# Output projection of a decoder layer: seven block products in place of eight, and three smaller edits around it

## The chip, the cores and the metric

The kernel runs on one core of one Trainium2 chip. The metric is device time in microseconds (us). A core has a matrix engine (PE, TensorE; the profile shows its weight loads apart, as PEld), a vector engine (DVE, VectorE), an activation engine (ACT, ScalarE), a general engine (POOL, GpSimd) and a queue engine for transfers (SP). Each works through its own queue of instructions in order and waits on semaphores for what the others produce.

## The reference

One decoder layer over 16 sequences of 256 tokens with 256 features, in f32. First a recurrent mixing block (an input product, a short convolution, a gated scan over time), then cross-attention with 8 heads of 128 columns, then a router with experts. The part that matters here is the cross-attention of one sequence, whose keys and values come from 256 latent rows (the normalised tokens themselves) and 77 context rows, 333 in all:

```python
q = x_n @ Wq + bq                      # 256 x 1024, 8 heads of 128
k, v = split(kv_in @ Wkv + bkv)        # 333 x 1024 each
p = softmax(q_h @ k_h.T / sqrt(128))   # per head, 256 x 333
o_h = p @ v_h                          # per head, 256 x 128
y = concat(o_h) @ Wo + bo + x          # 256 x 256: the output projection
x2 = layernorm(y)                      # goes to the router and the experts
```

The output projection is a product of 256 x 1024 by 1024 x 256.

## The kernel before

**Tiling and stages.** Stage A is the recurrence (`rec_in`, `rec_state`, `rec_add`, `rec_out`), for batches in pairs or fours. Stage B is the cross-attention, head by head. Stage C is the expert part, from about 1040 us on. A prologue loads weights, normalises the context and prepares batch 0.

**The loop over heads.** Stage B is one loop over 128 heads (16 batches by 8). Iteration i issues keys and queries of head i (`head_kq`, L573), then a list of extra steps for this (batch, head), then the product of scores and values of head i-2 (`head_out`, L624), the scores and softmax of head i (`head_softmax`, L589), the turning of the scores of head i-1 (`head_turn`, L608: TensorE transposes L617, copied by VectorE at L619 and by ScalarE at L620), and a second list of steps. A step of the first list is entered by `at(b, h, step, ...)`, one of the second by `behind(b, h, step, ...)`. These lists hold everything that is not a head: recurrence products, preparation of the next batch, projection, normalisation, router. A scheduler keeps dependences and decides from this order how each engine's queue is laid out; `tc.issue_after(x)` makes what is issued in its block come after x.

**The projection.** The head outputs of a batch are kept transposed in `ot` (128 x 8 heads x 256 tokens). For a batch b-1, `project` (L643) runs at (b, 2) for tokens 0 to 127 and at (b, 3) for tokens 128 to 255. Each half is 8 f32 products, one for each head, summed in half of one PSUM bank `pw`: the weights are the 128x128 block of `ot`, the moving operand is `wo_s[:, h, :]` of 256 columns (L649). In hardware one f32 product is two pairs of weight load and matmul, so a batch has 32 pairs. After the second half, GpSimd has added the bias to the tokens (`xb`, L663), VectorE adds `pw` and `xb` into `y` (L665), and `layernorm` (L139) takes its statistics and writes the normalised rows back into `xs` (L150). In batch 15, whose projection comes after the last head, each half is normalised by itself (`norm_half`).

**The neighbours that the change touches.** `prep_norm` (L487) makes the normalised rows `zl` of the next batch: four small GpSimd operations give the scale, then two VectorE operations (L492) multiply. It stands at (b, 2) for even next batches and (b, 0) for odd ones. `prep_keys` (L495) transposes `zl` and writes `kvt` (L506). `prep_values` (L533) already computes the values with seven products over blocks, in banks `pv`. `settle` (L686) scales a finished batch into `o` and sends it out. In the recurrence, `rec_in` convolves `hp` into `cv` (L336 to L338), takes its tanh into `th` (L341), and multiplies (L343). `load_rest` (L287) loads the projection's weights `wo_s`, 1 MB, by one transfer on SP in the prologue. Pools named b1, b2, a2 give tiles of one or two buffers.

Of the kernel before, what the change touches and what calls it, by code (L numbers as in the profile page):

```python
# [10 lines left out]
F32 = mybir.dt.float32  # L11
I32 = mybir.dt.int32
AF = mybir.ActivationFunctionType
ALU = mybir.AluOpType
# [4 lines left out]
P = 128  # L19
B, S, D = 16, 256, 256  # L20
# [6 lines left out]
KC = 4  # L27
H, DH = 8, 128
# [10 lines left out]
def decoder_layer(  # L39
# [28 lines left out]
    nc = tc.nc  # L68
    V, A, G, T = nc.vector, nc.scalar, nc.gpsimd, nc.tensor

    PB = 2
    PT = PB * S
# [11 lines left out]
    def bank(name, tag="mm", bufs=2):  # L84
        return ps.tile([P, 512], F32, tag=tag, bufs=bufs, name=name)
# [27 lines left out]
    part = cpool.tile([P, 2], F32, tag="part", name="part")  # L113
# [25 lines left out]
    def layernorm(dst, src, n, rows, name):  # L139

        mv = small.tile([P, n, 2], F32, tag="mv", name=f"mv{name}")
        for i in range(n):
            st = small.tile([P, 6], F32, tag="st", name=f"st{name}_{i}")
            V.bn_stats(st[:rows], src[:rows, i, :])
            V.bn_aggr(mv[:rows, i, :], st[:rows])
        v = small.tile([P, n], F32, tag="v", name=f"v{name}")
        V.tensor_scalar(v[:rows], mv[:rows, :, 1], EPS, None, ALU.add)
        r = rsqrt(v, n, rows, name)
        for i in range(n):
            V.tensor_scalar(  # L150
                dst[:rows, i, 0:D], src[:rows, i, :], mv[:rows, i, 0:1], r[:rows, i : i + 1], ALU.subtract, ALU.mult
            )
        return mv, r
# [28 lines left out]
    gl = wpool.tile([P, DC], F32, tag="gl", name="gl")  # L182
    bl = wpool.tile([P, DC], F32, tag="bl", name="bl")
    emb_s = wpool.tile([P, DC, E], F32, tag="emb", name="emb_s")
    wsum = wpool.tile([P, 4, 512], F32, tag="wsum", name="wsum")
# [126 lines left out]
    sums, yss, xs, stats = {}, {}, {}, {}  # L312

    def rec_in(pr, c, i=None):

        if c == 0 and pr > 0:
            hss[pr] = hs_tile(f"hs{pr}")
            sums[pr] = aw.tile([P, PT], F32, tag="sums", bufs=2, name=f"sums{pr}")
        a, n = (0, PB) if i is None else (i, 1)
        cols = slice(a * S, (a + n) * S)  # L320
        ph = bank(f"ph{pr}_{c}")[:, 0 : n * S]
        for k in range(DC):
            T.matmul(
                ph,
                lhsT=inw[:, k, c * P : (c + 1) * P],
                rhs=xTs[pr][:, k, cols],
                start=(k == 0),
                stop=(k == DC - 1),
            )
# [12 lines left out]
        hs = hss[pr]  # L342
        V.scalar_tensor_tensor(hs[:, c, cols], th, 1.0, z, ALU.add, ALU.mult)  # L343
# [51 lines left out]
    ysums, normed = {}, {}  # L395
# [25 lines left out]
    zs, kvts, vs, outs_t = {}, {}, {}, {}  # L421
# [62 lines left out]

    stages, kvt_ends = {}, {}

    def prep_norm(b):  # L487
# [153 lines left out]
    pws, norms, xbs = {}, {}, {}  # L641

    def project(b, i):  # L643

        ot = outs_t[b]
        if i == 0 or b == B - 1:
            pws[b] = bank(f"pw{b}_{i}")
        for h in range(H):
            T.matmul(  # L649
                pws[b][:, i * D : (i + 1) * D],  # L650
                lhsT=ot[:, h, i * P : (i + 1) * P],
                rhs=wo_s[:, h, :],
                start=(h == 0),
                stop=(h == H - 1),
            )
# [8 lines left out]
        y = b2.tile([P, 2, D], F32, tag="yb", name=f"yb{b}")  # L664
        V.tensor_tensor(y.rearrange("p i d -> p (i d)"), pws.pop(b), xb.rearrange("p i d -> p (i d)"), ALU.add)  # L665
        norms[b] = layernorm(xs[b], y, 2, P, f"b{b}")

    def norm_half(b, i):

# [24 lines left out]

    def settle_now(b):
        r2 = again(*norms.pop(b), f"o{b}")
        o = b2.tile([P, 2, D], F32, tag="yb", name=f"o{b}")
# [162 lines left out]
    for b in range(B):  # L860
        nb = b + 1
        new_pair = nb % PB == 0 and nb < B
        if b > 0:
            early = 2 * int(b == B - 1)
            at(b, 2, project, b - 1, 0)
            at(b, 3 - early // 2, project, b - 1, 1)
            at(b, 5 - early, turn_tokens, b - 1)
            at(b, 6 - early, score_experts, b - 1)
            at(b, 6 - early, choose, b - 1)
            at(b, 7 - early, dispatch, b - 1)  # L870
            at(b, 7, settle, b - 1)
        if new_pair:
            if nb == PB:
                at(b, 0, rec_state, nb, nb + 1)
            elif nb % 4 == 0:
                at(b, 0, rec_state, nb, nb + 3)
            at(b, 1, rec_add, nb, PB)
            at(b, 1, rec_out, nb)
            at(b, 2, prep_norm, nb)
            at(b, 3, rec_out, nb + 1)  # L880
            at(b, 3, prep_keys, nb)
            at(b, 3, prep_sums, nb)
            for n, h in enumerate((4, 6, 7)):
# [388 lines left out]
```

## Time and profile before

| what | value |
|---|---|
| median of 3 runs | 1182.75 us (1182.72 to 1184.29) |
| profiled execution, its own time | 1185.1 us |
| its span in the trace | 1183.4 us |
| PE busy | 1153.7 us, 5100 matmuls |
| weight loads busy | 830.1 us, 5100 loads |
| VectorE busy | 758.0 us, 2251 instructions |
| ScalarE busy | 486.7 us, 1284 instructions |
| GpSimd busy | 312.4 us, 564 instructions |
| matmuls of the projection (L649) | 512, a mean of 379 ns each from start to end |
| weight loads of the projection | 512, a mean of 190 ns each |

The profile is that of one execution, which lay 2.35 us above the median of the runs. "Busy" is the time in which an engine has at least one instruction under way; matmuls overlap, so the mean duration of one is longer than the distance from one to the next. A row of a group names the line, the engine, the operation, the tiles written and read, the shapes, the count, then busy time and the mean of one in ns, then the engine's idle time before them and who ended it. A row of a timeline gives the start of a run of equal instructions, the time from the first start to the last end, and their number; idle time before it stands in brackets.

### The profile page before, as it was taken

To read this page: it belongs to the slowest core of one execution; us is meant where nothing else is said; L and a number is where in the kernel's file an instruction comes from. 1 tells how busy PE (TensorE), PEld (TensorE's weight loads), DVE (VectorE), ACT (ScalarE), POOL (GpSimd) and SP (SyncE) were. 2 spreads that over 40 slices of the span, in tenths; PEclk is the share of its full clock that TensorE was granted. 3 is DMA by queue.
4 is the path that set the end of the run, shared out by engine and by line. 5 is a ranking of instruction groups with operands and counts; after the bars stand their busy time and mean duration, and the time that the engine had idled before them with its cause. 6 is when DMAs were issued, how large, how long until landed. Compare 5 with 4: busy or idle time off the path is not lost. (4 is left out here: it accounts for less than half of the span.)

```text
span 1183.4 us, 15727 instructions
## 1 busy us (share of the span) xinstructions
PE 1153.7 (97%) x5100; PEld 830.1 (70%) x5100; DVE 758.0 (64%) x2251; ACT 486.7 (41%) x1284; POOL 312.4 (26%) x564
## 2 busy tenths in 40 slices
PE   7999999999999999999999999999999999999996
PEld 3565677767777777677777777677777778876654
DVE  6655768676747674856467757756466564656665
ACT  3344444443444443444444434444344443523331
POOL 2211133222211321222113322222122212144544
PEclk9999999999999999999999999999999999999998
DMA  7740101000100010000000100000001000145752
GB/s 236 233 142 30 38 19 36 20 29 28 37 11 25 20 43 16 27 29 18 15 10 23 36 14 10 19 14 15 10 14 45 14 9 4 30 154 142 184 156 85
DMA packets 46617, 60.35 MB, mean 51 GB/s; under 512 B 7925, under 2 KB 36574, under 8 KB 46536
## 3 DMA queue, kind: packets, MB, share of 16 engines
q1 hardware_dynamic: 39158, 50.05, 13.4%
q0 software_dynamic: 6048, 9.22, 3.0%
q8 instruction: 40, 0.66, 0.2%
q14 instruction: 41, 0.34, 0.1%
q10 hardware_dynamic: 1330, 0.10, 0.1%
HBM read 36.07 MB, written 30.78 MB: 56 GB/s over the span
## 5 line engine op out<-in xcount | busy, mean ns | idle before, releaser
L631 PE MATMUL po<-ptt,v 128*128 128x256 f32 (+1 forms) x768 | 191.6, 383 | 1.5 <-DVE ptt L619 1.5
L631 PEld LDWEIGHTS po<-ptt,v 128*128 128x128 f32 (+1 forms) x768 | 141.8, 190 | 56.3 <-issue 29.8
L596 DVE TENSOR_REDUCE nm<-s 128x2 f32<-128x666 f32 x128 | 108.3, 846 | 93.1 <-PE s L594 93.1
L579 PE MATMUL pk<-kvt,wkv_s 128*128 128x333 f32 x512 | 164.9, 444 | 0.0
L594 PE MATMUL s<-kt,qt 128*128 128x333 f32 x512 | 164.3, 442 | 0.0
L600 ACT ACTIVATE p<-s,nm 128x333 f32<-128x333 f32 x256 | 135.3, 534 | 40.4 <-DVE nm L596 36.3
L639 ACT ACTIVATE ot<-po,bkv_s 128x256 f32<-128x256 f32 x128 | 60.6, 473 | 192.4 <-PE po L631 191.3
L584 PE MATMUL pq<-kvt,wq_s 128*128 128x256 f32 x512 | 131.2, 378 | 0.0
L579 PEld LDWEIGHTS pk<-kvt,wkv_s 128*128 128x128 f32 x512 | 91.1, 191 | 45.3 <-issue 22.5
L594 PEld LDWEIGHTS s<-kt,qt 128*128 128x128 f32 x512 | 96.4, 189 | 31.1 <-issue 0.5
L584 PEld LDWEIGHTS pq<-kvt,wq_s 128*128 128x128 f32 x512 | 96.7, 189 | 30.5 <-issue 0.5
L649 PE MATMUL pw<-wo_s,ot 128*128 128x256 f32 x512 | 115.9, 379 | 0.0
L620 ACT COPY ptt<-pb 77x256 f32<-77x256 f32 x128 | 47.0, 368 | 165.0 <-PE pb L617 162.3
L649 PEld LDWEIGHTS pw<-wo_s,ot 128*128 128x128 f32 x512 | 97.0, 190 | 13.2
L605 DVE TENSOR_SCALAR pn<-p,rs 128x333 f32<-128x333 f32 x256 | 100.0, 426 | 3.8
L835 POOL DMA_INDIRECT xg<-xs,sidx x64 | 65.4, 1022 | 92.4 <-DVE sidx L832 61.6
L619 DVE COPY ptt<-pa 128x512 f32<-128x512 f32 x128 | 87.1, 680 | 0.6 <-PE pa L617 0.6
L617 PEld LDWEIGHTS pa<-ident,pn 128*128 128x128 f32 x512 | 63.6, 141 | 31.4 <-DVE pn L605 3.5
L617 PE MATMUL pa<-ident,pn 128*128 128x128 f32 x512 | 78.3, 274 | 0.0
L581 ACT ACTIVATE kt<-pk,bkv_s 128x333 f32<-128x333 f32 x128 | 68.9, 538 | 22.0 <-PE pk L579 21.7
L338 DVE SCALAR_TENSOR_TENSOR cv<-hp,cw,cv 128x512 f32<-128x512 f32 (+1 forms) x108 | 73.8, 691 | 1.6
L663 POOL TENSOR_TENSOR xb<-xs,bo_s 128x256 f32<-128x256 f32 x30 | 19.8, 680 | 193.7 <-DVE yb L665 189.7
(231 smaller groups left out, 1686.3 us busy)
## 6 DMA issues: line engine op xcount, KB each, us to landing
v<-vc SPq DMA_DIRECT2D x16, 308.0 KB
xg<-zero SPq DMA_DIRECT2D x34, 131.0 KB
xe<-xg SPq DMA_DIRECT2D x8, 524.0 KB
xt<-in_x_in SPq DMA_DIRECT2D x16, 256.0 KB
out<-o SPq DMA_DIRECT2D x16, 256.0 KB
w<-in_w1T SPq DMA_DIRECT2D x8, 512.0 KB
w<-in_w2T SPq DMA_DIRECT2D x8, 512.0 KB
oe<-ye SPq DMA_DIRECT2D x15, 256.0 KB
```

The lines of the kernel that those rows point to most:

```text
L338: V.scalar_tensor_tensor(cv, hp[:, :, k : k + S], cw[:, c, k : k + 1], cv, ALU.mult, ALU.add)
L579: T.matmul(pk[:, 0:J], lhsT=wkv_s[:, k, f], rhs=kvt[:, k, :], start=(k == 0), stop=(k == DC - 1))
L581: A.activation(kt, pk[:, 0:J], AF.Identity, bias=bkv_s[:, h : h + 1])
L584: T.matmul(pq[:, 0:S], lhsT=wq_s[:, k, f], rhs=kvt[:, k, 0:S], start=(k == 0), stop=(k == DC - 1))
L594: T.matmul(s[:, ic, 0:J], lhsT=qt[:, ic * P : (ic + 1) * P], rhs=kt, start=True, stop=True)
L596: V.tensor_reduce(nm, s[:, :, 0:J], AX.X, ALU.max, negate=True)
L600: A.activation(p[:, ic, :], s[:, ic, 0:J], AF.Exp, bias=nm[:, ic : ic + 1], accum_out=sm[:, ic : ic + 1])
L605: V.tensor_scalar(pn[:, ic, :], p[:, ic, :], rs[:, ic : ic + 1], None, ALU.mult)
L617: T.transpose(dst[0:jn, c0 : c0 + P], pn[:, ic, j0 : j0 + jn], ident)
L619: turned = V.tensor_copy(ptt[:, 0:2, :], pt01.rearrange("p (j i) -> p j i", j=2))
L631: T.matmul(po[:, 0:S], lhsT=vs[b][0:jn, jc, h * DH : (h + 1) * DH], rhs=ptt[0:jn, jc, :], start=(jc == 0), stop=(jc == 2),)
L649: T.matmul(pws[b][:, i * D : (i + 1) * D], lhsT=ot[:, h, i * P : (i + 1) * P], rhs=wo_s[:, h, :], start=(h == 0), stop=(h == H - 1),)
```

## The change

- **Seven products.** For batches 0 to 13 the heads are taken as 4 pairs (e = 0, 1), the tokens as two blocks, and the columns of the weights as two blocks (n = 0, 1). For a pair this is a 2x2 by 2x2 product of 128x128 blocks, formed with 7 products in place of 8, as `prep_values` does for the values. All are summed over the 4 pairs in four quarters of one PSUM bank. Three products are formed at (b, 2), four at (b, 3).
- **Sums of the head outputs** (`project_sums`): two VectorE operations of 128x512 behind (b, 1) and two behind (b, 2), partly in place in `ot`.
- **Sums of the weights** (`project_weights`): four VectorE operations of 128x512 behind (0, 7). Three results go into the new tile `wosum`, one takes the place of block (0, 1) of `wo_s`.
- **Combining**: ScalarE copies three quarters of the bank (384 columns) into `u` after the first three products; VectorE adds two of its parts to the last 128 columns of `y`; after the last four products three more VectorE operations finish the sum, in place in `xb`. The old addition of 512 columns is gone.
- **Batches 14 and 15** keep the old `project`; `project_last` at (15, 0) loads the overwritten block of `wo_s` again (0.25 MB).
- **Order**: `zl` of `prep_norm` is issued after the last copy of turned scores (`turned`); the additions of `xb` on GpSimd are issued after `normed[b + 2]`.
- **Buffers**: `zl`, `o` have one buffer instead of two; the tanh is written into `hp` instead of a tile of its own; `y` is `xb`.

```diff
 def rec_in
-        z = cv.rearrange("p b s -> p (b s)")
-        th = a2.tile([P, PT], F32, tag="th", name=f"th{pr}_{c}")[:, 0 : n * S]
-        A.activation(th, z, AF.Tanh)
+        th = hp[:, :, KC - 1 :]
+        A.activation(th, cv, AF.Tanh)
...
 def prep_norm
-        zl = b2.tile([P, 2, D], F32, tag="zl", name=f"zl{b}")
+        zl = b1.tile([P, 2, D], F32, tag="zl", name=f"zl{b}")
         for i in range(2):
-            V.tensor_scalar(zl[:, i, :], xs[b][:, i, 0:D], r2[:, i : i + 1], None, ALU.mult)
+            if turned is None:
+                V.tensor_scalar(zl[:, i, :], xs[b][:, i, 0:D], r2[:, i : i + 1], None, ALU.mult)
+                continue
+            with tc.issue_after(turned.ins):
+                V.tensor_scalar(zl[:, i, :], xs[b][:, i, 0:D], r2[:, i : i + 1], None, ALU.mult)
...
+    wo_p = wo_s.rearrange("p (g e) f -> p g e f", e=2)
+    wo_block = lambda e, n: wo_p[:, :, e, n * P : (n + 1) * P]
+
+    def project_weights():
+        w = wo_block
+        t = lambda i: wosum[:, i, :, :]
+        V.tensor_tensor(t(0), w(0, 1), w(0, 0), ALU.subtract)
+        V.tensor_tensor(w(0, 1), w(1, 1), w(0, 1), ALU.subtract)
+        V.tensor_tensor(t(1), w(1, 1), t(0), ALU.subtract)
+        V.tensor_tensor(t(2), w(1, 0), t(1), ALU.subtract)
+
+    def project_last():
+        src = wo.rearrange("(g e p) f -> p g e f", p=P, e=2)
+        nc.sync.dma_start(wo_block(0, 1), src[:, :, 0, P:])
+
+    def project_sums(b, part):
+        x = lambda e, i: out_block(b, e, i)
+        if part == 0:
+            osums[b] = s = b1.tile([P, H // 2, P], F32, tag="osum", name=f"osum{b}")
+            V.tensor_tensor(s, x(0, 1), x(1, 1), ALU.add)
+            V.tensor_tensor(x(0, 1), x(0, 0), x(0, 1), ALU.subtract)
+            return
+        s = osums[b]
+        V.tensor_tensor(x(0, 0), s, x(0, 0), ALU.subtract)
+        V.tensor_tensor(s, x(1, 0), x(0, 0), ALU.subtract)
+
+    def project_pairs(b, part):
+        ...
+        if part == 0:
+            pws[b] = bank(f"pw{b}")
+            xbs[b] = xb = b1.tile([P, 2, D], F32, tag="xb", name=f"xb{b}")
+            with tc.issue_after(normed[b + 2].ins):
+                for j in range(2):
+                    G.tensor_tensor(xb[:, j, :], xs[b][:, j, 0:D], bo_s, ALU.add)
+            products = (0, x(0, 0), w(0, 0)), (1, osums[b], t(0)), (2, x(0, 1), w(0, 1))
+        else:
+            products = (3, x(0, 0), t(1)), (0, x(1, 0), w(1, 0)), (1, osums[b], w(1, 1)), (2, x(1, 1), t(2))
+        p = pws[b]
+        for r, lhsT, rhs in products:
+            for g in range(H // 2):
+                T.matmul(p[:, r * P : (r + 1) * P], lhsT=lhsT[:, g, :], rhs=rhs[:, g, :], ...)
+        xb = xbs[b]
+        y = xb.rearrange("p i d -> p (i d)")
+        if part == 0:
+            parts[b] = u = b1.tile([P, 3, P], F32, tag="u", name=f"u{b}")
+            A.copy(u.rearrange("p r d -> p (r d)"), p[:, 0 : 3 * P])
+            for r in (1, 2):
+                V.tensor_tensor(y[:, 3 * P :], y[:, 3 * P :], u[:, r, :], ALU.add)
+            return
+        u = parts.pop(b)
+        V.tensor_tensor(u[:, 0, :], u[:, 0, :], p[:, 3 * P :], ALU.add)
+        V.tensor_tensor(y[:, 0 : 3 * P], y[:, 0 : 3 * P], p[:, 0 : 3 * P], ALU.add)
+        y3 = y[:, P:].rearrange("p (r d) -> p r d", d=P)
+        V.tensor_tensor(y3, y3, u[:, 0:1, :].broadcast_to([P, 3, P]), ALU.add)
+        norms[b] = layernorm(xs[b], xb, 2, P, f"b{b}")
...
 steps
-            at(b, 2, project, b - 1, 0)
-            at(b, 3 - early // 2, project, b - 1, 1)
+            if b < B - 1:
+                behind(b, 1, project_sums, b - 1, 0)
+                at(b, 2, project_pairs, b - 1, 0)
+                behind(b, 2, project_sums, b - 1, 1)
+                at(b, 3, project_pairs, b - 1, 1)
+            else:
+                at(b, 0, project_last)
+                at(b, 2, project, b - 1, 0)
+                at(b, 2, project, b - 1, 1)
...
+    behind(0, 7, project_weights)
```

In the settling of a batch, `o` comes from pool b1 instead of b2.

More of the change, by code (lines that the diff above doesn't have):

```diff
@@ L184, in decoder_layer @@
     emb_s = wpool.tile([P, DC, E], F32, tag="emb", name="emb_s")
+    wosum = wpool.tile([P, 3, H // 2, P], F32, tag="wosum", name="wosum")
     wsum = wpool.tile([P, 4, 512], F32, tag="wsum", name="wsum")
@@ L338, in rec_in @@
             V.scalar_tensor_tensor(cv, hp[:, :, k : k + S], cw[:, c, k : k + 1], cv, ALU.mult, ALU.add)
-        z = cv.rearrange("p b s -> p (b s)")
-        th = a2.tile([P, PT], F32, tag="th", name=f"th{pr}_{c}")[:, 0 : n * S]
-        A.activation(th, z, AF.Tanh)
+        th = hp[:, :, KC - 1 :]
+        A.activation(th, cv, AF.Tanh)
         hs = hss[pr]
-        V.scalar_tensor_tensor(hs[:, c, cols], th, 1.0, z, ALU.add, ALU.mult)
+        V.scalar_tensor_tensor(hs[:, c, cols].rearrange("p (b s) -> p b s", b=n), th, 1.0, cv, ALU.add, ALU.mult)
         if c > 0 and pr > 0:
@@ L485, in decoder_layer @@
     stages, kvt_ends = {}, {}
+    turned = None
     def prep_norm(b):
         r2 = again(*stats.pop(b), f"z{b}")
-        zl = b2.tile([P, 2, D], F32, tag="zl", name=f"zl{b}")
+        zl = b1.tile([P, 2, D], F32, tag="zl", name=f"zl{b}")
         for i in range(2):
-            V.tensor_scalar(zl[:, i, :], xs[b][:, i, 0:D], r2[:, i : i + 1], None, ALU.mult)
+            if turned is None:
[3 more added lines that the diff above has]
+                V.tensor_scalar(zl[:, i, :], xs[b][:, i, 0:D], r2[:, i : i + 1], None, ALU.mult)
         zs[b] = zl
@@ L663, in project @@
             G.tensor_tensor(xb[:, j, :], xs[b][:, j, 0:D], bo_s, ALU.add)
-        y = b2.tile([P, 2, D], F32, tag="yb", name=f"yb{b}")
-        V.tensor_tensor(y.rearrange("p i d -> p (i d)"), pws.pop(b), xb.rearrange("p i d -> p (i d)"), ALU.add)
-        norms[b] = layernorm(xs[b], y, 2, P, f"b{b}")
+        flat = xb.rearrange("p i d -> p (i d)")
+        V.tensor_tensor(flat, pws.pop(b), flat, ALU.add)
+        norms[b] = layernorm(xs[b], xb, 2, P, f"b{b}")
+    wo_p = wo_s.rearrange("p (g e) f -> p g e f", e=2)
@@ new lines, in decoder_layer, with out_block @@
+    osums = {}
+    def out_block(b, e, i):
+        return outs_t[b].rearrange("p (g e) s -> p g e s", e=2)[:, :, e, i * P : (i + 1) * P]
+    def project_sums(b, part):
[8 more added lines that the diff above has]
+        V.tensor_tensor(s, x(1, 0), x(0, 0), ALU.subtract)
@@ new lines, in project_pairs @@
+    def project_pairs(b, part):
+        x = lambda e, i: out_block(b, e, i)
+        w = wo_block
+        t = lambda i: wosum[:, i, :, :]
+        if part == 0:
[10 more added lines that the diff above has]
+            for g in range(H // 2):
+                T.matmul(
+                    p[:, r * P : (r + 1) * P],
+                    lhsT=lhsT[:, g, :],
+                    rhs=rhs[:, g, :],
+                    start=(part == 0 and r == 0 and g == 0),
+                    stop=(g == H // 2 - 1),
+                    skip_group_check=True,
+                )
+        xb = xbs[b]
[11 more added lines that the diff above has]
+        V.tensor_tensor(y3, y3, u[:, 0:1, :].broadcast_to([P, 3, P]), ALU.add)
+        norms[b] = layernorm(xs[b], xb, 2, P, f"b{b}")
@@ L668, in norm_half @@
+    parts = {}
     def norm_half(b, i):
@@ L696, in settle_now @@
         r2 = again(*norms.pop(b), f"o{b}")
-        o = b2.tile([P, 2, D], F32, tag="yb", name=f"o{b}")
+        o = b1.tile([P, 2, D], F32, tag="yb", name=f"o{b}")
         for j in range(2):
```

## The prediction

> **What bounds the kernel now.** I read the page first (busy time, then the wait totals of TensorE), next the windows by stage, and last the timelines of TensorE, its weight loads and VectorE around one projection.
>
> ```profile
> PE 1153.7 (97%) x5100; PEld 830.1 (70%) x5100; DVE 758.0 (64%) x2251; ACT 486.7 (41%) x1284; POOL 312.4 (26%) x564
> ...
> 50.00:146.00 96.00, 95.23 (x377) 58.08 (x376) 62.80 (x137) 44.17 (x112) 14.55 (x34) 1.00 0.28 84
> 392.00:637.00 245.00, 243.20 (x1122) 179.95 (x1121) 160.58 (x446) 106.28 (x287) 60.28 (x115) 1.00 0.07 22
> ...
> PE po L631 <- DVE ptt L619: 1.5, 4, 0.4
> ```
>
> The first line is busy time over the span, the next two are windows (width, then PE, weight loads, DVE, ACT and POOL busy, granted clock, DMA), the last a row of TensorE's waits (total, times, longest). From 50 us to about 1040 us TensorE runs at 99% and full clock: in 392 to 637 only 1.8 of 245 us are free, while VectorE has 84 us free. So any TensorE time taken out of these stages comes out of the span one for one, as long as nothing else becomes late; and VectorE is the engine to watch, since its waits are the only ones TensorE shows there.
>
> **Part 1: seven products for eight.** The projection of a batch is two halves of 8 heads; an f32 product is two hardware pairs of weight load and matmul, so 32 pairs of 256 columns. After: 7 products x 4 pairs of heads x 2 = 56 pairs of 128 columns.
>
> ```profile
> 146.62 3.62 PE L649 MATMUL pw<-wo_s,ot 128*128 128x256 f32 x16
> ...
> 425.86 0.60 PE L617 MATMUL pa<-ident,pn 128*128 128x128 f32 x4
> 426.30 0.38 PE L617 MATMUL pb<-ident,pn 128*77 128x128 f32 x2
> ...
> 428.29 1.08 PEld L733 LDWEIGHTS pl<-emb_s,x 128*128 128x128 f32 x8
> 429.29 0.30 PEld L544 LDWEIGHTS pv<-wsum,tsum 128*128 128x128 f32 x2
> ```
>
> These are timelines: start, length from first start to last end, count. A single L649 matmul lasts 0.379 us by its group row and they overlap, so one follows the other after (3.62 - 0.379)/15 = 0.216 us: 32 x 0.216 = 6.91 us a batch. What a 128-column pair costs has two readings. Transposes of 128 columns: four start at 425.86 and the next group at 426.30, so 0.44/4 = 0.110 us. But they are single-pass transposes with the normalised scores as the weights; the nearest real f32 products that are bound by their weight loads are the 8-column ones of L733: eight loads start at 428.29, the next group at 429.29, and the first is held behind a 256-column matmul (0.216), so (1.00 - 0.216)/7 = 0.112 us. I take 0.112, since the new products also need a fresh 128x128 load for each 128 columns: 56 x 0.112 = 6.27 us. Saved: 6.91 - 6.27 = 0.64 us a batch, times 14 batches = **-8.9 us**. At 0.109 it is -11.3. Note how thin this is: 1/8 fewer multiplications should give 12.5% of 97 us = 12 us; the shorter matmul leaves the load (0.112) above the streaming (0.108), which eats a quarter of it. Each ns of pitch is 56 x 14 = 0.78 us.
>
> Here the Trainium skill speaks against the change. "TensorE: Matmul & The Clock Gate", Part 3 under "What overlaps and what doesn't", says that a weight load overlaps matmuls in flight only when it goes to another row group. Every load here takes all 128 rows, so by that rule a pair would cost load and stream in turn, 0.109 + 0.112 = 0.221 us: 12.4 us a batch, or +77 us over 14. The rows say otherwise: the L649 pairs, full 128x128 loads of 0.190 us each by their group row, follow at 0.216 with TensorE full, and L617 at 0.110, so those loads lie under the matmul before. The row decides. The same page's "Back-to-back issue gap" gives about 81 ns for a sustained load-and-matmul stream of 128 columns against some 56 isolated; that factor on 0.109 would be 0.159 us, 8.9 us a batch, +28 us (an estimate from that page). The 0.110 is already a stream of both, so I don't apply it; no 56-pair run of real f32 products of 128 columns stands in this trace, so it stays as a rival.
>
> **Part 2: VectorE's and ScalarE's added work.** Per batch VectorE gets four sums of 128x512 (0.68 each, by L515's row below), two adds of 128x128 (about 0.28), one of 128x128 from PSUM (0.29), two of 128x384 (about 0.55 each, between the 0.42 of 256 elements at L677 and the 0.69 of 512 at L665), and loses L665: 2.72 + 0.56 + 0.29 + 1.10 - 0.69 = 4.0 us, 56 us in all (758 to 814). ScalarE gets a copy of 384 from PSUM, about 0.5 us.
>
> ```profile
> L665 DVE TENSOR_TENSOR yb<-pw,xb 128x512 f32<-128x512 f32 x15 | 10.4, 691 | 46.1 <-PE pw L649 46.1
> ...
> L677 DVE TENSOR_TENSOR yl<-pw,xb 128x256 f32<-128x256 f32 x2 | 0.8, 424 | 3.8 <-PE pw L649 3.8
> ...
> L515 DVE TENSOR_TENSOR wsum<-wkv_s 128x512 f32<-128x512 f32 x1 | 0.7, 677 | 0.0
> ```
>
> Does it fit at heads 1 to 3? In batch 6 VectorE is idle from 456.4 to 462.8 (0.06 us busy in 6.4), then busy 5.82 of 8 us from 464 and 7.00 of 8 from 472. The first sums belong to the end of head 1, into the idle stretch. The second pair may overwrite its inputs only when products 0 and 1 have been read, and the two adds of u wait for ScalarE's copy: both wait at the front of VectorE's queue at the head's end, where what comes behind them is the next maximum of the scores (L596) and the copy of the turned scores (L619), for which TensorE waits. Idle time of 2 us before L665 (470.5) shows room at that place; the window from 472 is where it is tight. I cost it at nothing, with -1 to +6 us for the range: 0.4 us late in every batch would be 14 x 0.4 = 5.6.
>
> **Part 3: norm's rows behind the turned copy.** Now VectorE does work at head 3 for which nobody waits yet (the two zl operations in odd batches, the recurrence's in even ones) ahead of pn or ptt, for which TensorE waits. The change moves zl behind the copy of the turned scores.
>
> ```profile
> 478.49 1.53 PE L631 MATMUL po<-ptt,v 128*128 128x256 f32 x6 [0.40 <-DVE ptt L619]
> ...
> 544.63 0.84 PE L617 MATMUL pa<-ident,pn 128*128 128x128 f32 x4
> ```
>
> The first is batch 6's stall (0.4 to 0.56 us, also in batches 2 and 10); the changed program's instruction order puts that copy and the maximum before the recurrence's operations, some 0.7 us earlier: about -1.7 us in three batches. The second is batch 7: four transposes take 0.84 us instead of the 0.60 above, because pn comes late; about 0.185 us in six odd batches, -1.1. Against it, the xb adds now stand in POOL's queue ahead of the four small operations behind which zl waits (2 x 0.68 = 1.4 us): in batch 7 its transposes are still ready about 1.5 us before their turn by the same order. In batch 1, where the stall before was 0.45, I walk the copy of head 2 to 1.6 us late: +1.1. About +0.7 in all for small delays of 0.1 to 0.3 us elsewhere. Sum **-1.0 us**; range -2.8 to +6 together with part 2.
>
> **Part 4: the four weight operations in the prologue.** By the order of VectorE's instructions the first of them stands ahead of the first kvt (L506), the other three ahead of the second value sum (L556).
>
> ```profile
> 29.68 0.39 SPq L287 DMA_DIRECT2D wo_s<-in_wo  x1
> ...
> 37.57 1.00 DVE L506 TENSOR_SCALAR kvt<-pt,gl,bl 128x256 f32<-128x256 f32 x2 [0.23 <-PE pt L504]
> ...
> 43.43 0.69 DVE L554 TENSOR_TENSOR v<-v,pv 128x512 f32<-128x512 f32 x1
> ...
> 44.17 1.98 PE L544 MATMUL pv<-wsum,tsum 128*128 128x512 f32 x4
> ```
>
> The wo_s transfer, 1 MB issued at 29.68 behind 0.57 MB of others at some 240 to 350 GB/s, should land near 38; so the first waits to there and kvt moves from 37.6 to about 39. That alone is covered: TensorE has context products (L469) until 41.44. But the 4 x 0.68 = 2.7 us, 0.5 to 1 of it in VectorE's gaps (0.31, 0.40, 0.66 before L469's copies and L150), push L554, which frees the bank that TensorE takes at 44.17, from 44.1 to about 46.0: **+1.9 us**. TensorE is 99% busy from 50 to 146, so it is not given back. Range +0.5 (all in gaps) to +3 (none).
>
> **Covered edits.** The reload of 0.25 MB for the last two batches stands in SP's order between batch 15's v load and batch 13's output, so it starts once batch 13's last products have read the block (head 3 of batch 14) and is needed at head 2 of batch 15: 7 heads of at least 5 us each (TensorE's rows at the end) cover it, with DMA 7% busy; behind it on SP stands only that output. Were the cover gone, 0.25 MB at those rates and the issue would cost about 3 us. The tanh in place, zl, o and y in single buffers: the same operations, and their reuse lies a batch (61 us) apart; nothing. The tail from 1040 us (expert stage, chain on xg and xe) shifts as a whole.
>
> **Sum.** -8.9 - 1.0 + 1.9 = -8.0: the span 1183.4 becomes 1175.4, the profiled execution 1185.1 becomes 1177.1. The median of the runs, 1182.75, is 2.35 below the profiled one: 1174.75.
>
> **The rivals.**
> *A pair of 128 columns costs more than 0.122 us* (the other side). There the saved 6.91 - 56 p just pays the +0.9 of parts 3 and 4. For it: this trace has no such stream of f32 products, and the page's two rules; against it the 0.110 and 0.112. At 0.125 the time is 1185; at 0.159, 1182.75 + 28 + 0.9 = 1211; at 0.221, 1260. Chance 0.12, with 0.02 for a larger stall on VectorE.
> *VectorE becomes late in each batch.* For it: 7.00 of 8 us busy at head 3, three new waits in its queue. Against it: 6.3 us idle at head 1. At 0.5 to 0.7 us a batch, 7 to 10 us cancel the gain: 1182 to 1185. Chance 0.10.
> *The gain is larger.* Pitch 0.109 (-11.3), the prologue's cost in gaps (+0.5), the stalls gone (-1.8): 1182.75 - 12.6 = 1170. Chance 0.16.
> *The forecast* itself, 1172 to 1180: 0.60.
>
> **How the numbers follow.** 0.2% of 1182.75, 2.4 us, is about what a measurement of this kernel can tell from no change. Faster: 0.60 + 0.16 = 0.76; same, 1180.4 to 1185.1: 0.10; slower 0.14. The range leaves out the slower cases above 1185 and the lowest tip of the larger gain: 1169.5 to 1185.
>
> **What would show it.** Right: the new projection's matmuls follow at 0.110 to 0.113 us, 6.2 to 6.3 us a batch; TensorE's busy time near 1146; the value products at 44.17 now near 46; the 0.4 us stalls at batches 2, 6 and 10 and the 0.84 transposes gone; VectorE near 814. Wrong: a pitch over 0.12, waits of TensorE on ptt, pn or on the second sums of more than 0.5 us a batch, or an exposed wait for the reload at batch 15.

## The result and the profile after

The changed kernel takes 1174.59 us (median of 4 runs, 1173.69 to 1175.22) against 1182.74 us: the ratio is 0.9931, 95% interval 0.9914 to 0.9948, or 8.15 us less. Measured again in another group of runs beside before: 0.9939 (0.9926 to 0.9952). The prediction was 1174.75 us, in a range of 1169.5 to 1185.

First the busy line of the page after, then rows of TensorE's waits (total, times, longest, in us) of the same kernel.

```profile
PE 1140.7 (97%) x5436; PEld 833.5 (71%) x5436; DVE 812.1 (69%) x2367; ACT 494.5 (42%) x1298; POOL 321.2 (27%) x564
```

```profile
PE po L639 <- DVE rs L610: 1.6, 1, 1.6
...
PE pv L552 <- DVE v L562: 1.4, 1, 1.4
PE pt L512 <- DVE zl L500: 1.3, 1, 1.3
...
PE pw L729 <- DVE ot L705: 0.7, 1, 0.7
```

TensorE still bounds. VectorE has 54.1 us more (the working said 56), ScalarE 7.8 us more (14 x 0.5 = 7.0). TensorE's own busy time is 1140.7 us, where 1146 was forecast; it also depends on the clock of the execution, as shown below, so it does not measure the products alone. Each of the four rows comes once: one in the prologue (`pv`), three around batch 1. Of the four stalls on `ptt` before, those of batches 2, 6 and 10 are gone. That of batch 1 is not: it has grown from 0.29 to 1.64 us and is the first row here.

**The pair of 128 columns.** The timeline of TensorE after, at one second part of a projection (start, length, count):

```profile
154.91 1.05 PE L729 MATMUL pw<-wosum,ot 128*128 128x128 f32 x8
155.80 1.06 PE L729 MATMUL pw<-wo_s,ot 128*128 128x128 f32 x8
156.70 1.06 PE L729 MATMUL pw<-wo_s,osum 128*128 128x128 f32 x8
157.59 1.06 PE L729 MATMUL pw<-wosum,ot 128*128 128x128 f32 x8
158.48 0.60 PE L512 MATMUL pt<-ident,zl 128*128 128x128 f32 x4
```

Four groups of eight take 158.48 - 154.91 = 3.57 us: 0.1116 us a pair, where 0.112 had been taken. What a batch saves can be read in one where nothing else moves, batch 8, from the maximum of the scores (`nm`) of head 1 to that of head 4. Timelines of VectorE, before and then after:

```profile
578.71 0.84 DVE L596 TENSOR_REDUCE nm<-s 128x2 f32<-128x666 f32 x1
...
602.42 0.85 DVE L596 TENSOR_REDUCE nm<-s 128x2 f32<-128x666 f32 x1 [1.11 <-PE s L594]
```

```profile
574.81 0.85 DVE L604 TENSOR_REDUCE nm<-s 128x2 f32<-128x666 f32 x1
...
597.87 0.85 DVE L604 TENSOR_REDUCE nm<-s 128x2 f32<-128x666 f32 x1 [1.73 <-PE s L602]
```

23.71 us before, 23.06 after: 0.65 us less, where the working had 0.64. From the maxima of all heads, batches 4, 12 and 14 also save 0.65 to 0.66 us.

**Why the profiled spans differ by more.** They differ by 10.5 us (1183.4 to 1172.9), the medians by 8.15. Windows of before and of after (width, then PE, weight loads, VectorE, ScalarE and GpSimd busy, granted clock, DMA share, GB/s):

```profile
13.00:17.00 4.00, 4.00 (x9) 2.02 (x9) 3.59 (x10) 1.31 (x4) 1.50 (x3) 0.60 1.01 346
```

```profile
13.00:17.00 4.00, 4.00 (x12) 1.69 (x12) 4.00 (x13) 2.23 (x7) 2.12 (x4) 1.00 1.02 368
```

In the profiled execution of before the granted clock was 0.60 for these 4 us, which costs some 4 x 0.40 = 1.6 us (an estimate: TensorE was busy in all of them); in that of after it was 1.00. The changed kernel does not remove the dip: its second profile has 0.50 in the same window. So part of the 10.5 us is the chance of which execution was profiled. The prediction took 2.35 us off for that, which is just the difference between 10.5 and 8.15.

**The prologue.** VectorE and TensorE after:

```profile
36.21 0.69 DVE L684 TENSOR_TENSOR wosum<-wo_s 128x512 f32<-128x512 f32 x1 [0.65 <-DMA wo_s<-in_wo]
36.82 0.99 DVE L514 TENSOR_SCALAR kvt<-pt,gl,bl 128x256 f32<-128x256 f32 x2
...
43.14 0.68 DVE L687 TENSOR_TENSOR wosum<-wo_s,wosum 128x512 f32<-128x512 f32 x1
43.74 0.68 DVE L562 TENSOR_TENSOR v<-v,pv 128x512 f32<-128x512 f32 x1
```

```profile
42.32 0.72 PE L587 MATMUL pk<-kvt,wkv_s 128*128 128x333 f32 x2
44.47 1.98 PE L552 MATMUL pv<-wsum,tsum 128*128 128x512 f32 x4 [1.43 <-DVE v L562]
```

As worked out, the weight operations hold up the value sum, and TensorE waits for it. The transfer landed at 36.2 us and not 38, but it was also issued 1.8 us earlier than in the profile of before (27.9 in place of 29.68 us), which had the dip of the clock. From issue to landing it took 8.3 us, as had been taken. The wait is 1.43 us, not 1.9; in the second profile of the same kernel it is 1.83 us.

**Batch 1.** Timelines of TensorE after:

```profile
148.85 1.16 PE L729 MATMUL pw<-wo_s,ot 128*128 128x128 f32 x8 [0.69 <-DVE ot L705]
...
169.78 1.53 PE L639 MATMUL po<-ptt,v 128*128 128x256 f32 x6 [1.64 <-DVE rs L610]
...
201.90 0.81 PE L512 MATMUL pt<-ident,zl 128*128 128x128 f32 x4 [1.32 <-DVE zl L500]
```

With the pairs on either side of these waits set against their usual pitch the three cost 0.85, 1.80 and 1.48 us; the second stands in place of an old 0.45. Only the second was in the working, as 1.1 net.

### The profile page after: what moved, and what is told of

The parts are those of the page before. It is cut to its first block, busy times and chain, and to the rows that moved or that the text cites. A ratio compares the mean times of both kernels' runs of the same rounds, so it can differ in the third digit from the quotient of the medians.

```text
span 1172.9 us, 16419 instructions
## 1 busy us (share of the span) xinstructions
PE 1140.7 (97%) x5436; PEld 833.5 (71%) x5436; DVE 812.1 (69%) x2367; ACT 494.5 (42%) x1298; POOL 321.2 (27%) x564
## 5 line engine op out<-in xcount | busy, mean ns | idle before, releaser
L604 DVE TENSOR_REDUCE nm<-s 128x2 f32<-128x666 f32 x128 | 108.3, 846 | 54.3 <-PE s L602 54.1
L594 ACT ACTIVATE qt<-pq,bqs 128x256 f32<-128x256 f32 x128 | 61.0, 477 | 18.8 <-PE pq L592 14.9
L324 PE MATMUL ph<-xT,inw 128*128 128x512 f32 (+1 forms) x144 | 63.4, 570 | 5.0 <-DMA inw<-in_in_wT 4.9
L1183 PE MATMUL pf<-w,it 128*128 128x256 f32 x272 | 61.3, 381 | 2.7 <-ACT ye L1193 1.5
```

Source lines behind the costliest of these rows:

```text
L604: V.tensor_reduce(nm, s[:, :, 0:J], AX.X, ALU.max, negate=True)
L1183: T.matmul(po[:, 0:D], lhsT=it[:, f, s * P : (s + 1) * P], rhs=w2[:, f, :], start=(f == 0), stop=(f == NF - 1),)
```

## The experiments

Every time is set against before in the same group of runs, and each group ran on another chip. Before itself was 1182.8 us in the first group and 1175.4 in the two later ones (the section on the hardware says where that lies), so ratios are what to compare. The first four rows are the first group, the next four the second, the last three the third.

| kernel | us, and before beside it | ratio (95%) |
|---|---|---|
| edits alone, old projection | 1191.5, 1182.8 | 1.0075 (1.0052 to 1.0097) |
| changed, zl as before | 1201.8, 1182.8 | 1.0147 (1.0119 to 1.0174) |
| changed, weights later | 1172.5, 1182.8 | 0.9912 (0.9891 to 0.9933) |
| batch 0 by eight | 1173.2, 1182.8 | 0.9914 (0.9894 to 0.9934) |
| before, eight products split | 1179.3, 1175.5 | 1.0029 (1.0017 to 1.0042) |
| changed, sums twice | 1178.6, 1175.5 | 1.0028 (1.0017 to 1.0039) |
| before, zl moved alone | 1174.75, 1175.5 | 0.9995 (0.9987 to 1.0002) |
| edits alone, y apart | 1174.85, 1175.5 | 0.9999 (0.9990 to 1.0009) |
| changed, again | 1168.0, 1175.4 | 0.9939 (0.9926 to 0.9952) |
| zl as before, xb late | 1173.7, 1175.4 | 0.9988 (0.9980 to 0.9996) |
| mended | 1165.95, 1175.4 | 0.9924 (0.9908 to 0.9939) |

**The price of the pair by itself.** Before, with each product split in two of 128 columns:

```diff
+            for n in range(2) if b < B - 2 else ():
+                T.matmul(
+                    pws[b][:, i * D + n * P : i * D + (n + 1) * P],
+                    lhsT=ot[:, h, i * P : (i + 1) * P],
+                    rhs=wo_s[:, h, n * P : (n + 1) * P], ...)
```

> The kernel before, with the eight products of batches 0 to 13 each split into two of 128 columns: 64 pairs of 128 columns in place of 32 of 256, nothing added to VectorE. It measures the price of the pair by itself. Theory: 64 x 0.112 = 7.17 us a batch against 6.91: 1182.8 + 14 x 0.26 = 1186.4. Rival (loads not under the matmuls, 0.221 us): 14.1 us a batch, 1284; with 0.159 us: 10.2 us a batch, 1229.

Measured: +3.8 us (1179.3 against 1175.5), and TensorE's timeline shows

```profile
456.49 3.73 PE L650 MATMUL pw<-wo_s,ot 128*128 128x128 f32 x32
460.06 1.88 PE L323 MATMUL ph<-xT,inw 128*128 128x512 f32 x4
```

32 pairs in 3.57 us, 0.1116 us each. Both rivals about the pair (0.159 and 0.221 us) fall: the full-height weight loads lie under the matmul before. That the load sets the pace is read from the products of 8 columns, which follow at the same 0.112 us; it costs 0.004 us over half of the 256-column pitch (0.108).

**Zl moved alone, on the kernel before.**

```diff
-            V.tensor_scalar(zl[:, i, :], xs[b][:, i, 0:D], r2[:, i : i + 1], None, ALU.mult)
+            if turned is None:
+                V.tensor_scalar(...)
+                continue
+            with tc.issue_after(turned.ins):
+                V.tensor_scalar(...)
```

> The kernel before with the two zl operations behind the turned copy and nothing else. Theory as the prediction costed it: the six stalls of 0.185 us in odd batches go, 1182.8 - 1.1 = 1181.7, or 1183.2 if the 1.5 us wait for zl before batch 2 comes with it. Rival, after the run of the edits alone: the stall of 1.19 us at the turned copy in odd batches comes from the moved zl itself: 1182.8 + 7 = 1190.

Measured: no change that can be told (-0.7 us). The two effects named are both there. Timeline of TensorE at head 4 of batch 3, and a row of its waits:

```profile
296.92 0.60 PE L623 MATMUL pa<-ident,pn 128*128 128x128 f32 x4
```

```profile
PE po L637 <- DVE ptt L625: 1.5, 4, 0.4
PE pt L510 <- DVE zl L498: 1.3, 1, 1.3
```

The transposes take 0.60 us again (0.84 before), so the stalls of the odd batches are won: 0.3 us a batch by the maxima of the heads, more than the 0.185 taken. The wait for zl before batch 2 comes with it, 1.28 us with nothing else changed. And the four stalls on `ptt` stay at 1.5 us: moving zl does not remove them.

**The edits alone.** The changed kernel with the old projection, without the sums of the weights:

```diff
-            if b < B - 1:
-                behind(b, 1, project_sums, b - 1, 0)
-                at(b, 2, project_pairs, b - 1, 0)
-                behind(b, 2, project_sums, b - 1, 1)
-                at(b, 3, project_pairs, b - 1, 1)
-            else: ...
+            at(b, 2, project, b - 1, 0)
+            at(b, 3 - early // 2, project, b - 1, 1)
```

> The changed kernel with the old projection (eight products of 256 columns) in every batch, without the weight sums and the reload; the moved zl, the single buffers and the tanh in place stay. Theory: these edits by themselves remove the 0.56 us stalls at batches 2, 6 and 10 (1.7 us) and the 0.185 us ones of six odd batches (1.1 us), and bring the new wait for zl before batch 2 (1.3 to 1.5 us): 1182.7 - 2.8 + 1.4 = 1181.3, between 1180 and 1182. Rival: the stalls went because the shorter projection moved the work around them; then these edits alone give 1182 to 1185.

Measured: 8.7 us slower than before; both expectations missed. A row of its waits, and the timelines of VectorE, TensorE and GpSimd at head 4 of batch 3:

```profile
PE po L638 <- DVE rs L609: 7.2, 9, 1.0
```

```profile
296.82 1.22 DVE L150 TENSOR_SCALAR xs<-xt,mva,ra 128x256 f32<-128x256 f32 x2 [0.94 <-POOL ra L136]
297.96 0.68 DVE L626 COPY ptt<-pa 128x512 f32<-128x512 f32 x1
```

```profile
298.78 1.53 PE L638 MATMUL po<-ptt,v 128*128 128x256 f32 x6 [1.03 <-DVE rs L609]
```

```profile
295.40 0.72 POOL L670 TENSOR_TENSOR xb<-xs,bo_s 128x256 f32<-128x256 f32 x1
296.08 0.70 POOL L136 TENSOR_TENSOR ra<-va,nhalf 128x2 f32<-128x2 f32 x1
```

The norm of a later batch stands in front of the turned copy on VectorE and waits there for GpSimd's `ra`; TensorE then waits for `ptt` (the profile puts the wait down to `rs`, the small operation right behind the copy). GpSimd had an addition of `xb` of 0.72 us just ahead of `ra`. Six of the nine waits, 1.03 us each, are of this kind, in the odd batches; the other three are the old stalls of batches 2, 6 and 10. In the kernel before, the additions ran ahead of everything:

```profile
290.50 1.32 POOL L663 TENSOR_TENSOR xb<-xs,bo_s 128x256 f32<-128x256 f32 x2 [12.13 <-DVE yb L665]
```

There `xb` came free as soon as L665 had read it. With `y` in place in `xb` it comes free only when the rows have been normalised out of it. That was tested with `y` in its own tile. In the kernel before, `y` and `o` take turns in two buffers, so the test also gives `o` its second buffer back:

```diff
-        flat = xb.rearrange("p i d -> p (i d)")
-        V.tensor_tensor(flat, pws.pop(b), flat, ALU.add)
-        norms[b] = layernorm(xs[b], xb, 2, P, f"b{b}")
+        y = b2.tile([P, 2, D], F32, tag="yb", name=f"yb{b}")
+        V.tensor_tensor(y.rearrange("p i d -> p (i d)"), pws.pop(b), xb.rearrange("p i d -> p (i d)"), ALU.add)
+        norms[b] = layernorm(xs[b], y, 2, P, f"b{b}")
...
-        o = b1.tile([P, 2, D], F32, tag="yb", name=f"o{b}")
+        o = b2.tile([P, 2, D], F32, tag="yb", name=f"o{b}")
```

> The edits alone (old projection in every batch), but y keeps its own tile beside xb, and two buffers. Theory now: with y in place, the additions of xb for the next batch can't run before the rows are normalised out of xb; they stand on GpSimd in front of the scale of the next batch's norm, and the norm on VectorE stands in front of the turned copy: 1.19 us in each of six odd batches. With y apart this goes: 1191.5 - 7.1 = 1184.4. Rival (the moved zl or the tanh in place does it): 1191.

Measured: 0.9999 of before, so the whole 0.75% is gone and the cause is shown: the single buffers of `y` and `o`. That it is `y` and not `o` is read from the trace of the edits alone, where the additions of `xb` stand ahead of `ra` and `o` is written only at 299.58, behind it; no run separates the two. (The 1184.4 expected was for the level of the first group; it is 1.001 of before.) What is left, the tanh in place and the buffers of zl, costs nothing that can be told.

**The changed kernel with zl as before.** Here only the moved zl is undone:

```diff
-            with tc.issue_after(turned.ins):
-                V.tensor_scalar(zl[:, i, :], xs[b][:, i, 0:D], r2[:, i : i + 1], None, ALU.mult)
+            V.tensor_scalar(zl[:, i, :], xs[b][:, i, 0:D], r2[:, i : i + 1], None, ALU.mult)
```

> The changed kernel with the two zl operations issued as before, not behind the turned copy. Theory: the stalls of the odd batches come back (6 x 0.185 = 1.1 us), those at batches 2, 6 and 10 perhaps (1.7), and the wait of 1.3 us for zl before batch 2 goes: 1174.6 + 1.1 - 1.3 + (0 to 1.7) = 1174.4 to 1176.1. Rival: with 4 us more on VectorE in each batch the old order costs more than it did before, 0.4 us and more a batch: 1180 or above.

Measured: 1201.8 us, 27 us above the changed kernel. That is slower than even the rival had it, but not for the rival's reason. A row of TensorE's waits and VectorE's timeline at head 4 of batch 3:

```profile
PE pa L620 <- DVE pn L608: 16.5, 7, 2.8
```

```profile
302.25 0.15 DVE L605 RECIPROCAL rs<-sm 128x2 f32<-128x2 f32 x1
306.54 0.35 DVE L495 TENSOR_SCALAR zl<-xs,rlz 128x256 f32<-128x256 f32 x1 [4.14 <-POOL rlz L136]
306.81 0.69 DVE L608 TENSOR_SCALAR pn<-p,rs 128x333 f32<-128x333 f32 x2
```

But VectorE is not loaded here: it is idle for 4.14 us, held by zl, which waits for GpSimd, while `pn`, ready to go, stands behind it. GpSimd's timeline says what `rlz` came after:

```profile
301.11 0.72 POOL L717 TENSOR_TENSOR xb<-xs,bo_s 128x256 f32<-128x256 f32 x1
...
302.14 0.68 POOL L717 TENSOR_TENSOR xb<-xs,bo_s 128x256 f32<-128x256 f32 x1
...
304.90 0.94 POOL L780 TENSOR_SCALAR o<-xs,rlo 128x256 f32<-128x256 f32 x2
305.81 0.69 POOL L136 TENSOR_TENSOR rlz<-u3z,nhalf 128x2 f32<-128x2 f32 x1
```

So GpSimd's queue should be the cause. The waits of 16.5 us are not the whole 27 us: in five of the six odd batches TensorE's clock falls behind the wait. The section on the hardware shows it.

The test leaves VectorE's order as it is and moves only the additions of `xb` behind `rlz`:

```diff
-            with tc.issue_after(normed[b + 2].ins):
+            with tc.issue_after(powers[-1].ins):
                 for j in range(2):
                     G.tensor_tensor(xb[:, j, :], xs[b][:, j, 0:D], bo_s, ALU.add)
```

> The changed kernel with zl issued as before, and the two additions of xb on GpSimd issued behind the last scale (rlz) in place of the next norm's. Theory: the 2.93 us stall in six odd batches is zl, which stands in front of pn and waits for rlz, behind two xb additions (1.4 us), a settled output (0.9) and the places (0.5) on GpSimd; with rlz ahead of them the stall falls to about 0.2 us, so 6 x 2.7 = 16 us less than with zl as before: 19 - 16 = 3 us above the kernel before (1.002 to 1.004 of it). Rival (the stall is VectorE's load): 1.012 or more.

Measured: 0.9988 of before; 1.6% of the time is back. The row of waits is now

```profile
PE pa L620 <- DVE pn L608: 2.1, 6, 0.4
```

16.5 us of waits became 2.1. GpSimd's order is shown to be the cause. What remains is 0.9 us in each of the six odd batches by the maxima of the heads (0.2 was expected): zl in front of pn without the 1.4 us of additions. That is 5.4 of the 5.7 us by which this kernel lies above the changed one.

**Is there room on VectorE?**

```diff
             V.tensor_tensor(s, x(0, 1), x(1, 1), ALU.add)
+            V.tensor_tensor(s, x(0, 1), x(1, 1), ALU.add)
...
         V.tensor_tensor(s, x(1, 0), x(0, 0), ALU.subtract)
+        V.tensor_tensor(s, x(1, 0), x(0, 0), ALU.subtract)
```

> The changed kernel with one operation of each pair of sums of the head outputs done twice: 0.68 us more on VectorE at the end of head 1 and again at the end of head 2, 19 us in all. Theory (VectorE has room there): within 3 us of the changed kernel, 1174.6 to 1177.6, most of it in batch 1. Rival (VectorE is at its limit at these heads): half or more of the added time shows, 1184 and above.

Measured: 1.0028 of before, where the changed kernel is at 0.9939: 10.5 us more for 19 us of added work. The theory's 3 us is wrong. Rows of its waits:

```profile
PE pw L731 <- DVE ot L706: 6.0, 6, 1.0
...
PE pw L731 <- DVE osum L705: 2.1, 6, 0.5
```

Six times, and these are the six odd batches from 3 on, which by the maxima of the heads take 1.8 to 2.1 us more each, for 1.36 us of added work; the even batches lose nothing. How tight it was without the doubling is in the timelines of the changed kernel, VectorE and then TensorE, at head 2 of batch 3:

```profile
279.88 0.68 DVE L705 TENSOR_TENSOR ot<-ot 128x512 f32<-128x512 f32 x1
```

```profile
280.61 1.16 PE L729 MATMUL pw<-wo_s,ot 128*128 128x128 f32 x8
```

The second sum ends at 280.56, and its products start at 280.61. In batch 1, where they are held up, they also start 0.05 us after the sum's end (148.80 and 148.85), so in batch 3 there is no room left. The groups of eight start 0.92 us apart here, in place of 0.89. In batches 5 and 9 the sum ends some 0.26 us before its products.

**The weights later.**

```diff
+        with tc.issue_after(turned.ins):
             V.tensor_tensor(t(0), w(0, 1), w(0, 0), ALU.subtract)
...
-    behind(0, 7, project_weights)
+    behind(0, 4, project_weights)
```

> The four weight operations are issued behind head 4 of batch 0 (behind the turned copy there) in place of the prologue, where VectorE is idle for some 2.5 us. Theory: the wait of 1.43 us of TensorE for the second value sum in the prologue goes: 1174.6 - 1.4 = 1173.2. Rival: that wait is given back later, or the operations cost as much at their new place: 1174.6 within 1 us.

Measured: 1172.5 us, 2.1 less than the changed kernel's first median; the intervals overlap, so the trace has to say it. The row of waits for `pv` is gone and no other took its place, while the three waits of batch 1 are the same to 0.01 us. The wait was the weights' and is not given back. (The profiled span itself is not shorter, 1173.4 against 1172.9 us: this execution had a clock of 0.57 from 13 to 17 us, the changed kernel's 1.00.)

**Batch 0 by eight, and a mended version.** The first keeps the old projection for batch 0 and moves the weights behind head 5 of batch 1; the second splits the weight operations, three behind head 4 of batch 0 and the one that overwrites a block behind head 5 of batch 1. The edit of the second:

```diff
+            if b == 1:
+                at(b, 2, project, b - 1, 0)
+                at(b, 3, project, b - 1, 1)
-            if b < B - 1:
+            elif b < B - 1:
...
+    behind(0, 4, project_weights)
+    behind(1, 5, project_block)
```

> As the kernel with the weights later, but batch 0 keeps eight products, so seven are used for 13 batches from batch 1 on, and the weight operations stand behind head 5 of batch 1. Theory: the first sums cost the stalls of batch 1 (0.85 at the first products, 1.80 at the turned copy of head 2, perhaps the 1.48 before zl), since the recurrence's work is thickest there; without them and the prologue's 1.43, less 0.64 of lost saving and with the old 0.45 back: 1174.6 - 1.4 - 2.65 + 0.64 + 0.45 = 1171.6, or 1170.2 if the zl wait goes too. Rival: the stalls come from the moved zl and not from the sums: 1173.8.

> Batch 0 by eight products, seven from batch 1 on; three of the weight operations behind head 4 of batch 0, the one that overwrites a block of the weights behind head 5 of batch 1. Theory: the 0.45 us that the four operations cost at head 6 of batch 1 go as well; against the changed kernel -1.4 (prologue) -2.65 (batch 1's sums) -1.5 (zl wait) +0.64 +0.9 = -4.0: 0.9897 of before. Rival: the waits only move: 0.993 of before, as the changed kernel.

Measured: 0.9914 and 0.9924, the fastest of all together with the weights later. Both medians lie about 2 us below the changed kernel and not 4; the intervals overlap, and batch 0 by eight can't be told from the weights later (0.9912). The stall at the first sums is gone in both. With batch 0 by eight the wait for zl goes too, but 1.36 us at the turned copy stay and 0.45 come at the weight operations' new place. In the mended version these 0.45 go and the wait for zl is back; rows of its waits:

```profile
PE po L639 <- DVE ptt L627: 1.2, 1, 1.2
PE pt L512 <- DVE zl L500: 1.1, 1, 1.1
PE pc L891 <- DVE on L882: 0.6, 1, 0.6
```

By the maxima of the heads, the mended version is 2.4 us ahead of the changed kernel's second profile before batch 1 begins and 2.3 us ahead after batch 3: batch 1's waits only moved, and what it gains is the prologue. Here the rival was right for one half. What holds the turned copy in batch 1 was not isolated by a run; the section on the hardware has a likely part of it.

**The changed kernel again**, which gives the level for the later groups:

> The changed kernel once more, on the chip and beside the runs of before that the next two are measured with: 0.9931 of before as at first, or 8 us less. Both theories expect the same of it; it is the level for the doubled sums, for the zl as before with late additions, and for the mended version.

Measured: 1168.0 us, 7.3 less than before, as expected.

## Why the prediction was right, and where it was not

- **Seven products, -8.9.** Right, to 0.65 against 0.64 us a batch, by the row of the 8-column products and not by the rule that the prediction quotes from the Trainium skill ("TensorE: Matmul & The Clock Gate", Part 3, "What overlaps and what doesn't"): the overlap of loads and matmuls of the same rows is in the timelines above. (The figures of "Back-to-back issue gap" on the same page, as a factor on 0.109, give an estimate of 0.158 and not 0.159 us; nothing hangs on it.)
- **What bounds the kernel.** The reading that VectorE's waits are the only ones was not complete. Of the 1.8 us free from 392 to 637 us, 0.40 is the wait for `ptt`; 1.40 is a wait of the recurrence at 511.33 us for which the trace names no cause. It stands in both kernels, so the difference was not touched.
- **Weight operations, +1.9.** The mechanism and the place were right: the wait is 1.43 us in the first profile and 1.83 in the second, and vanishes when they are moved. The landing of `wo_s` at 38 us does not follow from the numbers written beside it: 1.57 MB at 240 to 350 GB/s from 29.68 us gives 34.2 to 36.2, and nothing is said of the rest. It was right all the same, as 8.3 us from issue to landing show. The 3 us for an uncovered reload hold such an unnamed part too: 0.25 MB at these rates and an issue of 0.39 us make 1.1 to 1.4 us.
- **VectorE's sums, at nothing.** Right for this kernel outside batch 1, but by luck: the step looked at batch 6, an even one, and found idle time. In batch 3 there is no room left. The rival of VectorE late in each batch was nearer than its 0.10 says.
- **The moved zl, -1.0.** The step that failed. As a sum over small stalls it was wrong in its parts. The odd batches' stalls are its own, and the wait for zl before batch 2 is too, but that wait is not in the sum: the working looked for room at batch 7 only. The stalls of batches 2, 6 and 10, put down to the same heading, stay when zl alone is moved and go only with the seven products. By the trace the waits of batch 1 are 3.7 us worse (0.85 + 1.80 + 1.48 - 0.45), not 1.1. Against them stand the removed stalls: 1.7 us in batches 2, 6 and 10, and by the maxima of the heads 2.6 us in the six odd batches, not 1.1. That these errors cancel is luck, and so is a total that came out this close.
- **The covered edits, at nothing.** Right for the tanh, and for the reload (no wait for it at batch 15). For `y` in place it was wrong as a statement about the edit: with the old projection the single buffers cost 8.7 us, since they delay when `xb` comes free. The working said that reuse lies a batch apart; it asked when the buffer is needed, and not where the instruction that waits for it stands in GpSimd's queue. In the changed kernel that cost does not appear. Two orders guard against it (`xb` behind the next norm, zl behind the turned copy); without the second the kernel takes 27 us more. The first was not undone by itself, so its worth is not shown.

So the time was right because the large term was measured well, the combination had no stall in the steady batches, and the errors in the small terms cancelled. The separate prices of the small edits were not right: they don't add.

## What to carry to other kernels

Price a pair of load and matmul from the nearest rows in the same trace, and look whether the load sets the pace: here products of 8 and of 128 columns both followed at 0.112 us. So 1/8 fewer multiplications gave 9% of the projection's time here. When a buffer is shared to save memory, look at which instruction now waits for it and what stands behind that one in its queue, on every engine; an idle engine with a ready instruction behind a waiting one looks like load, and isn't. Price an edit of order together with the edit that it protects: undoing the order of zl alone cost 27 us, over three times what the whole change brings.

## What the runs showed of the hardware that was not expected

**The clock after a wait.** The granted clock of TensorE dips at 12 to 19 us of some executions and not of others, for the same kernel. The changed kernel's first and second profile, its wait for the normalised context (total, times, longest), and the window of the second:

```profile
PE pt L444 <- DVE ctx L150: 2.0, 2, 1.6
```

```profile
PE pt L444 <- DVE ctx L150: 3.7, 2, 3.3
...
13.00:17.00 4.00, 4.00 (x9) 2.61 (x9) 4.00 (x14) 1.70 (x4) 0.98 (x3) 0.50 0.94 298
```

All 13 profiles divide in the same way. In five of them the longest of these waits is 1.6 to 1.9 us, and the clock from 13 to 17 us is 1.00. In the other eight it is 2.4 to 3.3 us, and the clock is 0.50 to 0.71. The maximum of head 0 of batch 0 lies at 54.10 us in the first profile and at 58.25 in the second. So a wait that is longer by chance is paid twice, and it can hide or feign a prologue change of 2 us.

The kernel with zl as before shows the same in its middle. TensorE waits 2.77 us for `pn` in batches 3, 5, 7, 9 and 11, and 2.26 us in batch 13. Behind five of these six waits the clock falls to 0.50 for some 3 us, as here after the wait that ends at 677.93:

```profile
678.00:680.00 2.00, 2.00 (x7) 1.57 (x8) 2.00 (x5) 0.35 (x2) 0.00 (x0) 0.50 0.63 176
```

In batch 3 it stays at 1.00. By the maxima of the heads that batch is 3.2 us longer than in the changed kernel, and the other five 4.4 to 5.1 us. So in this execution some 7.5 us are the lower clock (an estimate: the five against batch 3). No run changes a wait and nothing else, so that the wait brings the dip is read from these profiles and not tested. Nor does every wait bring one: the 4.85 us before TensorE's first product in the changed kernel's first profile are followed by a clock of 1.00.

**VectorE beside GpSimd.** The two operations of the norm at head 4 of the odd batches (L150, 128x256 each) take 0.77 us together in the kernel before, 1.22 us in the edits alone and 1.30 us in the changed kernel, where GpSimd's additions of `xb` run at the same time. In the kernel with zl as before and `xb` late, those additions run later, and the two operations take 0.77 us again. In batch 1 of the changed kernel they take 1.31 us, and the convolution behind them 1.12 in place of 0.75. These 0.91 us are a large part of what that stall grew by (0.29 to 1.64 us). For batch 1 this is read from the overlap in time and not tested.

**One chip and another.** The first group and the later groups differ by 7.4 us in the kernel before. In the first group the changed kernel's waits have

```profile
PE pp L385 <- issue: 3.9, 3, 1.3
```

and the later profile of the same kernel has no such row: for most of these waits the trace shows nothing that TensorE waits for (one of the three is put down to VectorE's zb in some profiles). Every profile of the first group has three of them, whatever the kernel, and none of the later groups. By the maxima of the heads the three recurrences take 1.7 us longer each, 5.1 us in all. The part behind the last head is longer too, 153.3 us on the mean of the first group's profiles and 150.3 on that of the others. The two together cover the 7.4 us. The groups ran on different chips; the cause is open.
